# Filter matmuls behind the last scan: single PSUM banks, and products and projections in runs of fixed order

## Chip, cores and metric

One Trainium2 chip, one of its cores. The metric is the device time of the kernel in microseconds (us), from the first to the last instruction. Engines are named as in the profile: PE (TensorE), ACT (ScalarE), DVE (VectorE), POOL (GpSimd), SP (the queue that issues all the DMAs here).

## What is computed

Two layers on x of shape 4 x 64 x 64 x 128, all in float32. Layer 0: a state-space block that scans each image in four directions, then a mixture of experts. Layer 1: a mixing of rows and columns, then a spectral filter. Only the last is touched. Cut to what matters:

```python
Vf = jnp.fft.rfft(phi, n=8192, axis=0)                  # 16 filters
Uf_p = jnp.fft.rfft(u, n=8192, axis=1)
Uf_m = jnp.fft.rfft(u * sgn3, n=8192, axis=1)
U_plus  = jnp.fft.irfft(Vf[None,:,:,None] * Uf_p[:,:,None,:], ...)[:, :sl]
U_minus = ... * sgn
out = jnp.einsum('btkd,k,kde->bte', U_plus, s, Mpp)     # projection per filter
out = out + jnp.einsum('btkd,k,kde->bte', U_minus, s, Mpm)
```

So for each of 4 images u (4096 x 128), sixteen causal convolutions, each followed by a 128 x 128 projection, and the sum of all that.

## The kernel before

**Stages.** The four images go one after another through a scan (the loop from L1308 on), which keeps DVE and POOL busy. Beside each scan, pieces of other work are dealt out, 24 of the 64 filter groups among them. The rest is done behind the last scan, in the *tail* (L1412 to L1440).

**The filter.** Time is cut into blocks of 32, and a transform over blocks (`to_slots`) turns the convolution into small independent products in 64 frequency slots. `convolve` (L1053) works on a *group* of four slots of one image. For each group there are four *parts*: two halves `kq` of the 16 filters, times `e` = 0 and 1 (even and odd outputs). A part loads one *slab* of filter windows (four DMAs of 256 KB, L1075) and makes eight *products* (L1097): 64 rows of contraction, so that slot `q` = 0 uses rows 0 to 63 of the PE array and `q` = 1 rows 64 to 127; 512 columns, a full PSUM bank each. A bank pair is copied to SBUF (`y0` or `y1`) by `evict` (L232), in the tail by DVE and ACT in turn. After both `e` of a half, sixteen *projections* (L1116, 128 rows, 512 columns) add up in one bank `zq_ps`: eight read `y0` (weights `me`), eight read `y1` (`mo`). I call this unit (two parts: 16 products and 16 projections) a *half-group*. After two of them POOL adds, PE transposes four times (L1138, `zt_ps`), and the result goes to DRAM for `from_slots` (L1163), which transforms back and writes the output.

**The tail.** 40 groups are left, 80 half-groups. Stage 1 of the tail runs 24 of them beside `first_stages` (the last image's `after_scans`, `experts_and_sums`, `to_slots`); stage 2 runs the last image's 16 groups beside `from_slots` of two images; then `from_slots` of the last image alone. The loop at L1433 takes a piece of the stage, adds its weight times a ratio (3.2 or 18) to `due`, and takes filter pieces until their weights reach `due`. A filter piece is what lies between two `yield`s of `convolve`: two products and a copy (weight 4), or one projection (weight 2).

**Order and buffers.** [...]that order is made by a list scheduler at build time, from dependencies and its own estimates: it moves PE instructions of the filter and of the other stage past each other. PSUM has eight banks; in the tail `slots(4, 2)` makes four single banks (`bank`) and two pairs (`pair`); the products use the pairs, everything else the singles. Slabs have two buffers (`cp` has bufs=2); part i+1's slab is loaded during part i.

Of the kernel before, what the change touches and what calls it, by code (L numbers as in the profile page):

```python
# [10 lines left out]
F32 = mybir.dt.float32  # L11
# [6 lines left out]
P = 128  # L18
# [23 lines left out]
BS = 32  # L42
NB = HALF // BS
NQ = NB
KQ = 8
# [31 lines left out]
def kernel(  # L77
# [127 lines left out]
    side = {"tail": False}  # L205

    def slots(ones, twos):
        if "pool" in side:
            side["pool"].close()
        side["pool"] = ExitStack()  # L210
        for name, n in (("ones", ones), ("twos", twos)):
            side[name] = n and side["pool"].enter_context(
                tc.tile_pool(name=f"side_{name}", bufs=n, space=PSUM)
            )

    def bank(shape, name):

        if side["ones"]:
            return side["ones"].tile(shape, F32, name=name, tag="ps")
        n = int(np.prod(shape[1:]))  # L220
        ap = pair(name)[0 : shape[0], 0, 0:n]
        if len(shape) == 2:
            return ap
        sizes = {f"d{i}": d for i, d in enumerate(shape[1:])}
        names = " ".join(sizes)
        return ap.rearrange(f"p ({names}) -> p {names}", **sizes)

    def pair(name):

        return side["twos"].tile([P, 2, 512], F32, name=name, tag="ps2")  # L230

    def evict(dst, src):  # L232

        side["n"] = side.get("n", 0) + 1
        if side["tail"] and side["n"] % 2:
            nc.vector.tensor_copy(dst, src)  # L236
        else:
            nc.scalar.copy(dst, src)  # L238
# [7 lines left out]
    def later(pieces, work):  # L246
        put_off.append([pieces, work])

    def tick():
        for item in list(put_off):  # L250
            item[0] -= 1
            if item[0] <= 0:
                put_off.remove(item)
                item[1]()
# [798 lines left out]
    def convolve(groups, pool=None):  # L1053


        if not side["tail"]:
            slots(0, 1)
        with tc.tile_pool(name="cv", bufs=2) if pool is None else nullcontext(pool) as cp:
            parts = [(b, G, kq, e) for b, G in groups for kq in range(KF // KQ) for e in range(2)]
            us, slab = {}, {}  # L1060

            def load(i):
                b, G, kq, e = parts[i]
                if kq == 0 and e == 0:
                    us[b, G] = cp.tile([P, 2, 2, C], F32, name="us")
                    nc.sync.dma_start(
                        us[b, G],
                        ud[b][4 * G : 4 * G + 4].rearrange("(p q) r s a c -> (q r s) p a c", p=2),
                    )

                slab[i] = cp.tile([P, 2, 2, KQ, 2 * BS], F32, name="slab")
                half = KQ * 2 * BS * 2
                for qr in range(4):
                    off = (4 * G * 2 + qr) * (HDQ // 2) + (kq * 2 + e) * half
                    nc.sync.dma_start(  # L1075
                        slab[i][qr * BS : (qr + 1) * BS].rearrange("s p r k x -> s p (r k x)"),
                        bass.AP(
                            hd.tensor, hd.offset + off, [[1, BS], [2 * HDQ, 2], [1, half]]
                        ),
                    )  # L1080

            load(0)
            yield LAG
            zt, ys = {}, {}
            for i, (b, G, kq, e) in enumerate(parts):
                if i + 1 < len(parts) and e == 0:
                    load(i + 1)
                y = cp.tile([P, 2, 4, 2, KQ, BS], F32, name=f"y{e}", bufs=1)
                ys[e] = y
                for a in range(2):  # L1090

                    off = 1 - a if e == 1 else 0
                    for p in range(2):
                        ps = pair("cv_ps").rearrange("p q (r k t) -> p q r k t", r=2, t=BS)
                        for q in range(2):
                            rows = slice(q * 2 * BS, (q + 1) * 2 * BS)
                            nc.tensor.matmul(  # L1097
                                ps[:, q],
                                us[b, G][rows, p, a if e == 0 else 1 - a, :],
                                slab[i][rows, p, :, :, off : off + BS],  # L1100
                                start=True,
                                stop=True,
                            )
                        evict(
                            y[:, a, 2 * p : 2 * p + 2].rearrange("p q r k t -> p q (r k t)"),
                            ps.rearrange("p q r k t -> p q (r k t)"),
                        )
                        yield 4.0
                if e == 0:
                    continue  # L1110
                z = bank([P, 2 * 4 * 2, BS], "zq_ps")
                for e in range(2):
                    if i + 1 < len(parts) and e == 1:
                        load(i + 1)
                    for k in range(KQ):
                        nc.tensor.matmul(  # L1116
                            z,
                            (me, mo)[e][:, KQ * kq + k, :],
                            ys[e][:, :, :, :, k, :].rearrange("p a q r t -> p (a q r) t"),
                            start=(e == 0 and k == 0),  # L1120
                            stop=(e == 1 and k == KQ - 1),
                        )
                        if not (e == 1 and k == KQ - 1):
                            yield 2.0
                zt[kq] = cp.tile([P, 2, 4, 2 * BS], F32, name=f"zt{kq}", bufs=1)
                evict(zt[kq].rearrange("p a q n -> p (a q n)"), z.rearrange("p n t -> p (n t)"))
                yield 2.0
                if kq == 0:
                    continue

                def gather(b=b, G=G, z0=zt[0], z1=zt[1]):
                    nc.gpsimd.tensor_add(z0, z0, z1)  # L1132

                    def turn():
                        ps = bank([P, 2, 2, C], "zt_ps")
                        for p in range(2):
                            for a in range(2):
                                nc.tensor.transpose(  # L1138
                                    ps[:, p, a, :],
                                    z0[:, a, 2 * p : 2 * p + 2, :].rearrange("e q n -> e (q n)"),  # L1140
                                    ident,
                                )
                        zo = cp.tile([P, 2, 2, C], F32, name="zo", bufs=1)
                        evict(zo, ps)
                        later(
                            4,
                            lambda: nc.sync.dma_start(
                                zd[b][4 * G : 4 * G + 4].rearrange(
                                    "(p q) r t a c -> (q r t) p a c", p=2
                                ),  # L1150
                                zo,
                            ),
                        )

                    later(3, turn)

                later(2, gather)
            yield LAG
            flush()
        if not side["tail"]:  # L1160
            slots(2, 0)
# [42 lines left out]
    def run(pieces):  # L1204
        for _ in pieces:
            tick()
        flush()
# [21 lines left out]
    with ExitStack() as c0:  # L1229
# [51 lines left out]
        traced = nc.cur_bb.bb.instructions  # L1281
        order = mybir.DependencyInfo(mybir.DependencyClass.NoSync, mybir.DependencyReason.DATA)
# [25 lines left out]
        for s in range(-5, total + 2):  # L1308
            i = max(s, 0) // N

            t = s + 5
# [8 lines left out]
            t = s + 3  # L1320
# [11 lines left out]
            if 0 <= s < total:  # L1332
                b, k, step, _ = chunks[i]
# [76 lines left out]


    side["tail"] = True  # L1412
    slots(4, 2)

    def first_stages():
        yield from after_scans(B - 1)
# [8 lines left out]
    with tc.tile_pool(name="cv_tail", bufs=2) as cp:  # L1425

        for stages, groups, ratio in (
            (first_stages(), all_groups[BESIDE * (B - 1) : last], 3.2),
            (back(), all_groups[last:], 18.0),
        ):  # L1430
            filtered = convolve(groups, cp)
            due = made = 0.0
            for weight in stages:  # L1433
                tick()
                due += weight * ratio
                while made < due:
                    made += next(filtered, 1e9)
                    tick()
            run(filtered)
    run(from_slots(B - 1))  # L1440
    side["pool"].close()

# [73 lines left out]
```

## Time and profile before

The time is 11827.28 us, median of 3 runs (11826.74 to 11830.04).

| | us |
|---|---|
| span of the profiled run | 11825.1 |
| last scan instruction group ends, tail begins | 9376 |
| tail stage 1 (first stages beside filters) | 9376 to 10858 |
| tail stage 2 (back transforms beside filters) | 10858 to 11780 |
| last back transform alone | 11780 to 11825 |
| PE matmul records in the whole span | 34144 |

A float32 matmul leaves two records (passes) on PE, so the 80 half-groups of the tail show 2560 records at L1097 and 2560 at L1116. "Busy" in the group view is the union of the records' durations; their ends are modelled and reach into the next record, so I also use the distance from a record's start to the next record's start on PE, which adds up to the span.

### The profile page before, as it was taken

To read this page: it belongs to the slowest core of one execution; us is meant where nothing else is said; L and a number is where in the kernel's file an instruction comes from. 1 tells how busy PE (TensorE), PEld (TensorE's weight loads), DVE (VectorE), ACT (ScalarE), POOL (GpSimd) and SP (SyncE) were. 2 spreads that over 40 slices of the span, in tenths; PEclk is the share of its full clock that TensorE was granted. 3 is DMA by queue.
4 is the path that set the end of the run, shared out by engine and by line. 5 is a ranking of instruction groups with operands and counts; after the bars stand their busy time and mean duration, and the time that the engine had idled before them with its cause. 6 is when DMAs were issued, how large, how long until landed. Compare 5 with 4: busy or idle time off the path is not lost. (4 is left out here: it accounts for less than half of the span.)

```text
span 11825.1 us, 115511 instructions
## 1 busy us (share of the span) xinstructions
PE 8573.0 (72%) x34144; PEld 4828.5 (41%) x34144; DVE 8088.6 (68%) x6718; ACT 6138.8 (52%) x11666; POOL 7497.5 (63%) x6710
## 2 busy tenths in 40 slices
PE   6676675545766777557677775676677799999998
PEld 2444343333443334434544334454343333444333
DVE  0898888976976889868879897797798612122221
ACT  4656666656465555564655555646556433133111
POOL 1787788988776777877867779777677630011001
PEclk9787787656876888668778785786888799999999
DMA  2464556565645566647456556474665654534444
GB/s 100 159 206 163 195 170 212 192 189 156 237 155 171 175 188 181 192 141 245 158 177 185 173 176 195 167 241 140 191 190 174 179 134 127 131 99 115 109 106 107
DMA packets 901449, 1980.03 MB, mean 167 GB/s; under 512 B 101562, under 2 KB 415578, under 8 KB 899290
## 3 DMA queue, kind: packets, MB, share of 16 engines
q1 hardware_dynamic: 900826, 1972.65, 55.0%
q8 instruction: 278, 4.55, 0.2%
q14 instruction: 345, 2.83, 0.1%
HBM read 1766.77 MB, written 205.52 MB: 167 GB/s over the span
## 5 line engine op out<-in xcount | busy, mean ns | idle before, releaser
L1364 POOL TENSOR_TENSOR hh<-hh,bc 128x1024 f32<-128x1024 f32 x2048 | 4827.7, 2358 | 478.0 <-DVE hh L1356 186.9
L1356 DVE TENSOR_TENSOR_SCAN hh<-da,hst,db 128x512 f32<-128x512 f32 x3584 | 4393.1, 1267 | 768.0 <-PE y L1390 362.2
L1390 PE MATMUL y<-ident,hh 128*128 128x128 f32 x16384 | 2862.3, 325 | 1502.4 <-POOL hh L1364 1365.3
L1325 ACT ACTIVATE da<-dl,aneg 128x512 f32<-128x512 f32 x4096 | 2768.5, 717 | 2148.5 <-DVE hh L1356 2120.3
L1390 PEld LDWEIGHTS y<-ident,hh 128*128 128x128 f32 x16384 | 2315.9, 168 | 2944.8 <-POOL hh L1364 1750.2
L1350 DVE TENSOR_TENSOR db<-du,bc 128x1024 f32<-128x1024 f32 x2048 | 2523.4, 1232 | 832.7 <-ACT du L1344 718.5
L1097 PE MATMUL cv_ps<-slab,us 64*128 64x512 f32 x4096 | 1397.7, 707 | 590.2 <-ACT y L238 218.9
L238 ACT COPY y<-cv_ps 128x1024 f32<-128x1024 f32 x700 | 704.3, 1007 | 1152.7 <-PE cv_ps L1097 1100.6
L236 DVE COPY y<-cv_ps 128x1024 f32<-128x1024 f32 x324 | 396.0, 1224 | 1252.7 <-PE cv_ps L1097 1218.5
L1116 PE MATMUL zq_ps<-y,me 128*128 128x512 f32 x2048 | 1021.5, 616 | 70.4 <-ACT y L238 59.9
L1363 POOL COPY hst<-hh 128x2 f32<-128x2 f32 x1792 | 338.6, 189 | 1103.8 <-DVE hh L1356 1009.4
L1116 PE MATMUL zq_ps<-y,mo 128*128 128x512 f32 x2048 | 976.0, 601 | 6.1 <-DVE y L236 4.8
L1097 PEld LDWEIGHTS cv_ps<-slab,us 64*128 64x128 f32 x4096 | 421.6, 206 | 1213.4 <-ACT y L238 370.4
L1132 POOL TENSOR_TENSOR zt<-zt,zt 128x512 f32<-128x512 f32 x64 | 81.0, 1266 | 955.8 <-ACT zt L238 528.6
L1356 DVE TENSOR_TENSOR_SCAN hh<-da,db 128x512 f32<-128x512 f32 x512 | 597.1, 1208 | 129.1 <-PE y L1390 57.0
L1255 PE MATMUL dt_ps<-dts,dtw 8*128 8x512 f32 x512 | 409.5, 901 | 276.0 <-ACT dl L1258 128.1
L385 PE MATMUL cv_ps<-xh,diag 128*128 128x512 f32 x1152 | 541.1, 613 | 1.4 <-ACT xh L378 1.4
L1116 PEld LDWEIGHTS zq_ps<-y,me 128*128 128x128 f32 x2048 | 349.4, 194 | 429.4 <-issue 342.7
L1116 PEld LDWEIGHTS zq_ps<-y,mo 128*128 128x128 f32 x2048 | 359.1, 192 | 313.4 <-issue 298.5
L1264 POOL TENSOR_TENSOR ex<-ex,dx 128x1024 f32<-128x1024 f32 x128 | 302.6, 2364 | 162.1 <-ACT dx L1263 162.1
L1194 POOL TENSOR_TENSOR xr<-xr,iv 64x256 f32<-64x256 f32 x128 | 88.6, 719 | 412.0 <-ACT iv L1189 318.8
L385 PEld LDWEIGHTS cv_ps<-xh,diag 128*128 128x128 f32 x1152 | 215.5, 198 | 223.0 <-issue 220.8
(217 smaller groups left out, 8720.1 us busy)
## 6 DMA issues: line engine op xcount, KB each, us to landing
bc<-bc_d SPq DMA_DIRECT2D x2048, 512.0 KB
slab<-hd SPq DMA_DIRECT2D x1024, 256.0 KB
xc<-xc_d SPq DMA_DIRECT2D x128, 512.0 KB
y_d<-ys SPq DMA_DIRECT2D x128, 512.0 KB
w1t<-in_w_dram SPq DMA_DIRECT2D x128, 512.0 KB
w2t<-in_w_dram SPq DMA_DIRECT2D x256, 256.0 KB
xc_x<-xc_d SPq DMA_DIRECT2D x64, 512.0 KB
yk<-y_d SPq DMA_DIRECT2D x128, 256.0 KB
```

The lines of the kernel that those rows point to most:

```text
L236: nc.vector.tensor_copy(dst, src)
L238: nc.scalar.copy(dst, src)
L385: nc.tensor.matmul(ps, diag[:, h, t, :], xh[:, 8 * g + dy : 8 * g + dy + 8, dx : dx + W], start=(t == 0), stop=(t == 8),)
L1097: nc.tensor.matmul(ps[:, q], us[b, G][rows, p, a if e == 0 else 1 - a, :], slab[i][rows, p, :, :, off : off + BS], start=True, stop=True,)
L1116: nc.tensor.matmul(z, (me, mo)[e][:, KQ * kq + k, :], ys[e][:, :, :, :, k, :].rearrange("p a q r t -> p (a q r) t"), start=(e == 0 and k = ...
L1255: nc.tensor.matmul(ps, dtw[:, k, h * P : (h + 1) * P], dts, start=True, stop=True)
L1325: i_act = nc.scalar.activation(das[t][:, h, :], sizes[t // N][0][:, h, :], AF.Exp, scale=aneg[:, tk, h, t % N : t % N + 1],)
L1350: nc.vector.tensor_mul(db, dus[i], bcs[s][:, 0:1, :].to_broadcast([P, 2, SC]))
L1356: i_dve = nc.vector.tensor_tensor_scan(o, d0, d1, init, ALU.mult, ALU.add)
L1363: nc.gpsimd.tensor_copy(hsts[t // N][:, :, t % N], hhs[t][:, :, last])
L1364: i_pool = nc.gpsimd.tensor_mul(hhs[t], hhs[t], bcs.pop(t)[:, 1:2, :].to_broadcast([P, 2, SC]))
L1390: i_pe = nc.tensor.matmul(ys[c][:, q, h, :], hhs[t][:, h, q * P : (q + 1) * P], ident, is_transpose=True, start=(n == 0 and k > 0 and q % ...
```

## The change

In the tail only (`side["tail"]`), the changed kernel

- makes all eight PSUM banks single (`slots(8, 0)`): a product takes one bank, and each bank is copied by itself (512 columns in place of 1024), by DVE and ACT in turn;
- gives the products weight 0, so that all eight of a part are emitted without anything of the other stage between them, and each projection weight 4;
- adds ordering edges on PE (`behind`): each filter instruction stands behind the filter instruction before it, and other stages' PE instructions behind the last filter instruction emitted before them, so the scheduler no longer reorders the filters;
- loads slabs two parts ahead, into three buffers;
- puts the transposes of a finished group off by 12 pieces in place of 3.

```diff
-                slab[i] = cp.tile([P, 2, 2, KQ, 2 * BS], F32, name="slab")
+                slab[i] = cp.tile(
+                    [P, 2, 2, KQ, 2 * BS], F32, name="slab", bufs=3 if side["tail"] else 2
+                )
...
             load(0)
+            if side["tail"]:
+                load(1)
...
-                if i + 1 < len(parts) and e == 0:
+                if side["tail"]:
+                    if i + 2 < len(parts):
+                        load(i + 2)
+                elif i + 1 < len(parts) and e == 0:
                     load(i + 1)
...
-                        ps = pair("cv_ps").rearrange("p q (r k t) -> p q r k t", r=2, t=BS)
+                        ps = None if side["tail"] else pair("cv_ps")
+                        pq = [bank([P, 512], "cv_ps") if ps is None else ps[:, q] for q in range(2)]
+                        to = y[:, a, 2 * p : 2 * p + 2].rearrange("p q r k t -> p q (r k t)")
...
-                        yield 4.0
+                        if side["tail"]:
+                            for q in range(2):
+                                evict(to[:, q], pq[q])
+                            yield 0.0
+                        else:
+                            evict(to, ps)
+                            yield 4.0
...
-                    if i + 1 < len(parts) and e == 1:
+                    if i + 1 < len(parts) and e == 1 and not side["tail"]:
                         load(i + 1)
...
-                            yield 2.0
+                            yield 4.0 if side["tail"] else 2.0
...
-                    later(3, turn)
+                    later(12 if side["tail"] else 3, turn)
...
-    slots(4, 2)
+    slots(8, 0)
+    last_pe = []
+
+    def behind(start, filters):
+        for ins in traced[start:]:
+            if ins.engine == mybir.EngineType.PE:
+                if last_pe:
+                    tc.add_manual_dep(ins, last_pe[-1], order, reason="queued behind")
+                if filters:
+                    last_pe.append(ins.name)
...
+            start = len(traced)
             for weight in stages:
                 tick()
+                behind(start, False)
+                start = len(traced)
                 due += weight * ratio
                 while made < due:
                     made += next(filtered, 1e9)
                     tick()
+                behind(start, True)
+                start = len(traced)
             run(filtered)
+            behind(start, True)
```

More of the change, by code (lines that the diff above doesn't have):

```diff
@@ L1097, in convolve @@
                             nc.tensor.matmul(
-                                ps[:, q],
+                                pq[q].rearrange("p (r k t) -> p r k t", r=2, t=BS),
                                 us[b, G][rows, p, a if e == 0 else 1 - a, :],
@@ L1103, in convolve @@
                             )
[L1104 to L1107, printed above, removed]
-                        yield 4.0
+                        if side["tail"]:
[5 more added lines that the diff above has]
+                            yield 4.0
                 if e == 0:
```

## The prediction

> **What bounds the kernel now.** I read the page first. Its second part, the span in 40 slices, has two regimes:
>
> ```profile
> PE   6676675545766777557677775676677799999998
> DVE  0898888976976889868879897797798612122221
> ...
> PEclk9787787656876888668778785786888799999999
> ```
>
> Up to slice 31 DVE is the busy engine (the scans). In the last eight slices PE is full, DVE little used, and PE's clock is whole. The order of the two built programs is the same on every engine up to that tail, so only the tail from 9376 us on is at stake, 2449 us. The busy times by stretch cut it at its stages; after the stretch and its length come PE, weight load, DVE, ACT, POOL, then clock, DMA share and GB/s:
>
> ```profile
> 9376.00:10858.00 1482.00, 1373.72 (x4667) 599.44 (x4668) 306.74 (x293) 463.33 (x1087) 235.57 (x469) 0.97 0.49 123
> 10858.00:11780.00 922.00, 882.97 (x2298) 331.81 (x2296) 184.28 (x164) 171.76 (x196) 65.82 (x81) 0.99 0.44 107
> 11780.00:11825.00 45.00, 21.84 (x32) 5.06 (x32) 0.00 (x0) 10.94 (x16) 22.05 (x32) 0.73 0.74 185
> ```
>
> PE is busy 93 to 96% in both stages, so only cheaper PE time can help. The groups of the tail say where it goes (busy, mean ns of one, idle before and its releasers):
>
> ```profile
> L1097 PE MATMUL cv_ps<-slab,us 64*128 64x512 f32 x2560 | 821.2, 643 | 100.8 <-ACT y L238 47.3 <-DVE y L236 34.1 <-DMA slab<-hd 17.9
> L1116 PE MATMUL zq_ps<-y,me 128*128 128x512 f32 x1280 | 606.8, 610 | 16.8 <-DVE y L236 10.1 <-ACT y L238 6.7
> L1116 PE MATMUL zq_ps<-y,mo 128*128 128x512 f32 x1280 | 573.3, 596 | 6.1 <-DVE y L236 4.8 <-ACT y L238 1.1
> ```
>
> From start to start, the products take 897 us, the projections 1164, all else 380: 2441. A projection record takes 0.43 us (16 of them from 11174.04 to 11181.00), and 2560 x 0.43 = 1101, so projections are near their floor. For the products I went to the timeline of PE (start, length, instructions, records):
>
> ```profile
> 9878.62 1.99 PE L1097 MATMUL cv_ps<-slab,us 64*128 64x512 f32 x8
> 9881.10 1.99 PE L1097 MATMUL cv_ps<-slab,us 64*128 64x512 f32 x8 [0.49 <-DVE y L236]
> 9883.56 2.10 PE L1097 MATMUL cv_ps<-slab,us 64*128 64x512 f32 x8 [0.47 <-DVE y L236]
> 9886.15 1.99 PE L1097 MATMUL cv_ps<-slab,us 64*128 64x512 f32 x8 [0.49 <-DVE y L236]
> ...
> 11191.63 2.02 PE L1097 MATMUL cv_ps<-slab,us 64*128 64x512 f32 x4
> 11193.58 1.12 PE L1116 MATMUL zq_ps<-y,me 128*128 128x512 f32 x2
> 11194.64 1.99 PE L1097 MATMUL cv_ps<-slab,us 64*128 64x512 f32 x8
> 11196.56 2.84 PE L1116 MATMUL zq_ps<-y,me 128*128 128x512 f32 x6
> ```
>
> Eight records (four products) take 1.92 us to the next start, and four records (two products) 1.95. In the eight, records start two at a time, 7 ns apart, then 0.53 and 0.43 us on: both row halves of the array work at once. In the four they start one after the other. The built order explains it: there the scheduler put two products of the same half together, then others, then two of the other half; 83 of the 312 product runs of the tail are such "aa" or "bb". And a long run stalls 0.5 us after every four products, with two bank pairs to write.
>
> **What the skill says.** "TensorEngine Tiling (Array Packing)", section Key Properties: tiles work independently, and changing the tiling mode drains the engine. The trace agrees with both: 7 ns between halves, and the start after a change between L1097 and L1116 comes after 0.52 us in place of 0.43, so 0.09 each. The same page, PSUM Bottleneck: a faster tiled PE can leave the copies as the bound, and ScalarE and VectorE should share them. "TensorE: Matmul & The Clock Gate", The cost: per-tile semaphore tail: each product that counts up a semaphore costs about 26 ns at the end of a set. The change doubles these counts; no run here shows that price, and at 1280 products it is at most 17 us for the 640 added.
>
> **The change, part by part.**
>
> *Products in runs of 16.* In the changed built order 79 of 80 half-groups have one run of 16, halves strictly alternating (one is cut into 2, 1 and 13). Eight pairs of two passes: 0.53 + 14 x 0.43 + 0.53 = 7.08 us; x 80 = 566. Removed: 897 - 566 = **331 us**.
>
> *Can the copies follow?* Copies of one bank are in the trace: `zt` 586 ns on ACT, 692 on DVE. Per pair of products (0.86 us) each of the two makes one, so 0.69 fits, with little to spare. Depth: a first product ends 1.12 us after the run starts (0.53 + 0.59), a copy follows some 0.1 later and is done by 1.95; the bank is wanted by the fifth pair at 3.5. The slack is 1.5 us. Copies of 512 cost more per column (two on ACT 1.17 against 1.01), but lie under 13.8 us of projections, in which no copy is due. In stage 2 I therefore book no wait. `y0` and `y1` have one buffer each: their last readers are the projections ahead of the run, done on PE before it, so no wait.
>
> *Projections.* 80 x 32 x 0.43 = 1101. They are now broken by stage instructions in some 270 places and by products in 80, x 0.09 = 32: 1133. Removed: 1164 - 1133 = **31 us**.
>
> *All else* stays in number: 380.
>
> *Slabs two ahead.* 2 MB per half-group in about 21 us is 100 GB/s, and 25 to 60 for the rest; the page shows up to 245 GB/s in a slice. A slab is asked for once the part before last is done, some 20 us ahead of use. SP stands behind the store of `zo` at times, which comes five projections into the next half-group; a slab's four issues take 1.7 us and it lands some 5 later (the chain has 5 to 7 us at `slab<-hd`), before the need. The 17.9 us of slab waits are mostly the first load (14.7 us at 9399), which stays. Booked at nothing, but not safe.
>
> *The added order.* A stage's PE instruction now stands at a fixed place among the projections; if its input is late, all filters behind it wait, and with them the copies and the next slabs. Before, the stage instructions of stage 1 waited for next to nothing (idle 0.0 at most of their lines). I book: 12 us where `to_slots` of the last image now stands alone between the stages (its 16 matmuls and the DMA round trip have no filter beside them in the built order; before, they were mixed); 9 us where DVE's `top` and `rest` (4.4 us each) stand between copies of one run; 25 us for about eight runs in which the norm sums of ACT (0.3 to 0.5 us each, a dozen or more) stand between the copies and use up the 1.5 us slack, 3 us each; 13 for slabs and semaphores. Together **59 us**.
>
> Sum: 11827 - 331 - 31 + 59 = 11524; I say **11525 us**, and 11465 if the 59 vanish.
>
> **Rivals.**
>
> *The copies or the order bind in stage 1.* For it: ACT is busy there 463 of 1482 us, in order, waiting on POOL for each norm, and filters now cannot be moved around a late input. Against: eight banks in place of two pairs, and nearly no stage waits before. If every one of the 48 half-groups of stage 1 loses 3 us more: 11525 + 144 = about 11670.
>
> *The DMA takes over.* For it: a slab now has 21 us in place of 26, experts' weights come in stage 1 beside it. Against: DMA share 0.44 to 0.49. At 26 us per half-group in stage 2 nothing of its 170 us (half of the gain) is left: about 11695.
>
> *The halves do not overlap* (slower). Each product now waits for its own bank; if the second half always started after the first had ended, 16 products would take 16 x 0.86 = 13.8 us, x 80 = 1101, 204 more than now: 11827 + 204 - 31 + 59 = about 12060. Against: pairs with waits on different semaphores for each product (both satisfied) already start 7 ns apart.
>
> *It comes out better than the sum*: stage waits of before (some 40 us in the 380) shrink too: about 11440.
>
> **Chances.** Forecast 0.74; stage 1 binds 0.13; DMA 0.05; halves apart 0.03; better 0.05. The range reaches from 11455 (the 59 gone, a little of the waits too) to 11640 (most of stage 1's rival). Faster 0.96, same 0.01, slower 0.03.
>
> **What would show it.** Right: L1097 with 2560 records at some 570 to 600 us from start to start, runs of 32 records in 7.1 us; a half-group of stage 2 in 21 to 22 us in place of 27; copies at 0.59 and 0.69; PE still above 93% in stage 2. Wrong: PE idle before L1097 for y copies of over 60 us (rival one), for slabs over 30 (two), records of L1097 0.43 apart singly (three). A PE clock below 0.95 in the tail would also break it.

## The result and the profile after

The changed kernel takes 11536.91 us (median of 4 runs, 11531.63 to 11545.08); the kernel before, on the same chip, 11828.66 us (11826.74 to 11833.45). The ratio is 0.9753, with a 95% interval of 0.9736 to 0.9770. Predicted were 11525 us (11455 to 11640). The page's slices after, the same three rows as before:

```profile
PE   6676676545666677646767776566767779999998
DVE  0898888886886889967878889688789962222222
...
PEclk9687787656777888767778887677788889999999
```

The picture is that of before, with the full-PE regime one slice shorter. Busy time by stretch (stretch, length, then PE, weight load, DVE, ACT, POOL, clock, DMA share, GB/s), cut where the first filter of stage 2 starts and at the last back transform:

```profile
9376.00:10761.00 1385.00, 1321.84 (x4800) 617.68 (x4800) 355.75 (x503) 492.58 (x1291) 242.05 (x473) 0.97 0.55 139
10761.00:11484.00 723.00, 715.89 (x2176) 302.57 (x2176) 193.45 (x280) 185.69 (x312) 64.40 (x80) 0.99 0.52 122
11484.00:11529.00 45.00, 22.27 (x32) 5.25 (x32) 0.00 (x0) 10.91 (x16) 22.04 (x32) 0.73 0.75 186
```

PE is now busy 95% of stage 1 and 99% of stage 2 (93 and 96% before), and the DMA share rose by the shorter time only (0.49 to 0.55, 0.44 to 0.52; over both stages the rates and times give the same bytes). Stage 2 is shorter by more than the rate says, because of where it is cut: in the changed kernel stage 1's half-groups are all done there, while before, 16 products and 32 projections of stage 1 and 21 of the 32 passes of `fu_ps` still lay behind the cut at 10858. The groups of the tail (busy, mean ns, idle before and its releasers):

```profile
L1127 PE MATMUL zq_ps<-y,me 128*128 128x512 f32 x1280 | 598.9, 605 | 2.5 <-DVE y L236 2.5
L1106 PE MATMUL cv_ps<-slab,us 64*128 64x512 f32 x2560 | 595.0, 607 | 40.7 <-ACT no_sq L277 14.3 <-DMA us<-ud 10.7 <-ACT zt L238 8.1
L1127 PE MATMUL zq_ps<-y,mo 128*128 128x512 f32 x1280 | 584.3, 598 | 0.2 <-ACT y L238 0.2
```

The 81 us of waits for `y` copies ahead of the products are gone from this list. What is left of the idle time ahead of the products is the tail's first product (14.3), the first after `to_slots` (10.7), and 15.7 us elsewhere. The timeline of PE in stage 2 shows what the products have become (start, length, records):

```profile
10988.28 7.18 PE L1106 MATMUL cv_ps<-slab,us 64*128 64x512 f32 x32
10995.39 5.42 PE L1127 MATMUL zq_ps<-y,me 128*128 128x512 f32 x12
11000.65 0.60 PE L1149 MATMUL zt_ps<-ident,zt 128*128 128x128 f32 x4
11001.08 1.88 PE L1127 MATMUL zq_ps<-y,me 128*128 128x512 f32 x4
11002.80 7.03 PE L1127 MATMUL zq_ps<-y,mo 128*128 128x512 f32 x16
11009.76 7.18 PE L1106 MATMUL cv_ps<-slab,us 64*128 64x512 f32 x32
...
11032.86 7.18 PE L1106 MATMUL cv_ps<-slab,us 64*128 64x512 f32 x32
```

Sixteen products, 32 records, then the next start 7.11 us on (10988.28 to 10995.39); a half-group takes 21.5 us (10988.28 to 11009.76, with the transposes of `zt_ps` in it) or 23.1 (to 11032.86, with `gi_ps` of `from_slots`), in place of about 27.

Added up over the tail from one record's start on PE to the next record's start:

| us | before | after | measured | predicted |
|---|---|---|---|---|
| products | 897.4 | 607.5 | -290 | -331, and +47 of added waits |
| projections | 1163.6 | 1143.7 | -20 | -31 |
| `fu_ps` (`to_slots`, the junction of the stages) | 9.8 | 36.3 | +27 | +12 |
| all other | 347.0 | 326.0 | -21 | 0 |
| sum | 2417.8 | 2113.5 | -304 | -303 |

The sum came out within 2 us, partly by luck: three of its terms were off and cancelled. One thing that the prediction had at nothing is spread over these rows: the trace shows stretches of the tail in which PE's granted clock is 0.50 in place of 1.00 and a pass takes 0.86 us in place of 0.43. They add up to 135 us before and 110 after, and half of PE's busy time in them, an estimate of what they cost, is 42.5 us before and 30.8 after; in the products alone 28.6 and 10.4. By that estimate some 12 of the 304 us come from the clock, in one profiled run each; what moves the clock is not shown here.

The span has another source of scatter: the last scan ends on PE at 9384.5 us before and 9393.4 after, and between 9381.5 and 9400.8 over all the kernels below, though nothing up to there was edited. From that point to the end the tail takes 2440.6 us before and 2135.9 after. I give this *tail* beside each time from here on; it comes from one profiled run each, while the times have intervals.

### The profile page after: what moved, and what is told of

It is laid out like the page before. It is cut to its first block, busy times and chain, and to the rows that moved or that the text cites. A ratio compares the mean times of both kernels' runs of the same rounds, so it can differ in the third digit from the quotient of the medians.

```text
span 11529.3 us, 116175 instructions
## 1 busy us (share of the span) xinstructions
PE 8359.0 (73%) x34144; PEld 4814.5 (42%) x34144; DVE 8136.4 (71%) x7038; ACT 6172.0 (54%) x11986; POOL 7488.7 (65%) x6710
## 5 line engine op out<-in xcount | busy, mean ns | idle before, releaser
L1106 PE MATMUL cv_ps<-slab,us 64*128 64x512 f32 x4096 | 1172.2, 684 | 542.0 <-ACT zt L238 196.1
L238 ACT COPY y<-cv_ps 128x512 f32<-128x512 f32 (+1 forms) x1024 | 755.4, 741 | 643.2 <-PE cv_ps L1106 614.2
L236 DVE COPY y<-cv_ps 128x512 f32<-128x512 f32 x640 | 441.8, 691 | 633.1 <-PE cv_ps L1106 599.0
L236 DVE COPY zt<-zq_ps 128x512 f32<-128x512 f32 x37 | 25.6, 691 | 493.4 <-PE zq_ps L1127 487.7
```

Source lines behind the costliest of these rows:

```text
L1106: nc.tensor.matmul(pq[q].rearrange("p (r k t) -> p r k t", r=2, t=BS), us[b, G][rows, p, a if e == 0 else 1 - a, :], slab[i][rows, p, :, : ...
```

## Experiments

The theory: the gain comes from PE's own time, because runs of 16 products with strictly alternating halves and a bank each keep both row halves of the array full, and the copies can just follow. Rivals for the cause: the banks alone do it, whatever the order; the fixed order alone does it; the slabs loaded earlier do it; the copies are in fact the limit. None of the kernels leaves out any of the work. Their numbers, with ratio and 95% interval against the kernel before on the same chip; "products" and `fu_ps` are start to start over the tail:

| kernel | time, us | ratio | tail | products | `fu_ps` |
|---|---|---|---|---|---|
| changed | 11536.9 | 0.9753 (0.9736 to 0.9770) | 2135.9 | 607.5 | 36.3 |
| e1_order_alone | 11737.7 | 0.9926 (0.9911 to 0.9940) | 2348.4 | 816.0 | 35.4 |
| e2_banks_alone | 11550.8 | 0.9768 (0.9752 to 0.9784) | 2159.0 | 659.8 | 10.9 |
| e3_slab_one_ahead | 11549.1 | 0.9765 (0.9750 to 0.9779) | 2161.9 | 623.0 | 35.9 |
| e4_turn_after_3 | 11545.8 | 0.9759 (0.9744 to 0.9773) | 2154.8 | 617.6 | 36.8 |
| e5_halves_apart | 11676.8 | 0.9874 (0.9854 to 0.9893) | 2287.3 | 766.1 | 35.6 |
| e6_copies_on_dve | 11521.8 | 0.9742 (0.9728 to 0.9757) | 2132.4 | 604.1 | 35.9 |
| e7_ratio_3 | 11511.3 | 0.9729 (0.9713 to 0.9746) | 2118.6 | 608.2 | 18.4 |
| e8_ratio_prime | 11498.2 | 0.9724 (0.9709 to 0.9738) | 2112.2 | 608.4 | 15.1 |
| e9_prime_dve | 11494.1 | 0.9716 (0.9702 to 0.9731) | 2104.3 | 604.3 | 15.1 |
| e10_banks_slabs | 11518.5 | 0.9737 (0.9720 to 0.9753) | 2127.9 | 629.3 | 10.8 |
| e11_prime_dve_free | 11520.7 | 0.9741 (0.9725 to 0.9757) | 2128.6 | 630.9 | 14.4 |

### The order alone

Against the kernel before: the pairs stay (`slots(4, 2)`, one copy of 1024 columns), slabs one ahead, transposes after 3 pieces; added are only the weights and the edges.

```diff
-                        yield 4.0
+                        yield 0.0
-                                yield 2.0
+                                yield 4.0 if side["tail"] else 2.0
+    def behind(start, filters):   # as in the change, called in the loop of the tail
```

> The changed kernel with the copies in bank pairs again (four singles, two pairs), slabs one part ahead and the transposes put off by 3: of the change only the fixed order and the weights are left. My theory (bank depth and adjacent halves both needed): a product run stalls some 0.5 us before every second pair, as the run at 9878 us did (9.45 us for 16 products), so 80 x (9.45 - 7.11) = 187 us over the changed kernel's 11537: about 11725. Rival 'the fixed order carries the gain': at most 11570. Rival 'the banks carry it all': about 11820.

Measured: 11737.7 us, tail 92 us shorter than before. The halves now alternate in every run (a run is a row of products with no other PE work between), but the two pairs hold the products up; its products:

```profile
L1101 PE MATMUL cv_ps<-slab,us 64*128 64x512 f32 x2560 | 696.4, 646 | 153.3 <-DVE y L236 66.4 <-ACT y L238 58.9 <-DMA slab<-hd 15.7
```

125 us of waits for copies (81 before). A run of 16 takes 9.50 us in place of 7.11; 42 half-groups have one, the other 38 have their run cut by transposes. So the long runs without the banks bring less than a third of the tail's gain.

### The banks alone

```diff
-    slots(4, 2)
+    slots(8, 0)
-                        ps = pair("cv_ps")...; evict(<both>, ps)
+                        pq = [bank([P, 512], "cv_ps") for q in range(2)]
+                        for q in range(2): evict(to[:, q], pq[q])
```

Old weights, no edges, slabs one ahead, transposes after 3 pieces.

> Eight single banks and copies of one bank only; weights, slabs, put-off and the scheduler's freedom as before. Its built order has 199 product runs in the tail, all of them strictly alternating between the halves, none of the 83 same-half runs of the kernel before. My theory (what counts is that both halves work at once, and that a run finds free banks): counted by slots of 0.86 us and 0.2 per run the products take 594 us against 568, so about 11537 + 26 + 0 to 20 = 11565 to 11585. Rival 'the fixed order carries the gain': 11750 or more.

Measured: 11550.8 us, better than expected; the tail is 281.6 us shorter than before, so the banks, with copies bank by bank, bring 92% of the 304.7 without the order. The order is not needed to keep the halves alternating: with single banks the scheduler left 199 product runs in the tail, of 1 to 16 products, and in each the halves alternate; all the "aa" and "bb" runs are gone, as the expectation had read from the built order. Why the scheduler makes them with pairs and not with single banks stays open. So does what it is about the banks that helps with the waits for copies: the products can now take any of eight banks in place of two pairs, and each bank comes free by itself; no run separates the two. Both edits, the banks and the order, remove the "aa" and "bb" runs, so their gains (92 and 282) don't add up.

### One slab ahead, and the transposes after 3 pieces

```diff
-                    ... name="slab", bufs=3 if side["tail"] else 2   # and load(i + 2)
+                    ... name="slab", bufs=2                          # and load(i + 1), as before
```

> The changed kernel with slabs in two buffers and loaded one part ahead, as before. My theory (a slab is asked for some 14 us before its use even so, and lands in about 5 to 7): within 15 us of 11537. Rival 'the two-ahead load is needed': product runs wait for slab DMA by 1 us or more each, 11620 or more.

```diff
-                    later(12 if side["tail"] else 3, turn)
+                    later(3, turn)
```

> The changed kernel with a group's four transposes put off by 3 pieces, not 12. In the built order they now stand inside a product run (after 6 of 16 products) in some 38 of 40 groups. My theory: each costs a break (0.2 us) and a wait for POOL's addition (1.3 us behind the copy of the last projections, about 2.5 us after the run starts, while six products take 2.7): 38 x 0.3 to 1 us, 11545 to 11575. Rival 'no effect': 11537 within 5.

Measured: 11549.1 and 11545.8 us; the first within the 15 us of its expectation, the second at the low end, and neither separated from the changed kernel by its interval alone. In the tails, +26 and +19 us. Of e3's, +15.5 lie in the products and +9 in the projections, a spread of small waits; the wait for slabs itself is small, and 14.8 us of it stand ahead of the tail's first product:

```profile
L1101 PE MATMUL cv_ps<-slab,us 64*128 64x512 f32 x2560 | 595.9, 607 | 51.8 <-DMA slab<-hd 18.6 <-ACT y L238 16.0 <-issue 10.3
```

18.6 us of slab waits, about what the kernel before had (17.9). So the loads are worth some tens of microseconds at most.

### Is it the overlap of the halves?

The same work on the same banks, but each part makes its four products of one half and then four of the other, and the copies follow in that order.

```diff
+                    for q in range(2):
+                        for a in range(2):
+                            for p in range(2): nc.tensor.matmul(banks[4 * q + 2 * a + p] ...)
```

> The changed kernel, but each part emits its four products of rows 0-63 first and its four of rows 64-127 then (aaaabbbb in place of abababab). Same records, same number of copies, same run length. My theory: equal halves in a row go one after the other, and only a change of half overlaps: a run takes about 11.2 us in place of 7.1, 80 x 4.1 = 328: about 11865, slower than before. Rival 'run length and banks, not the alternation': 11540 to 11560.

Measured: 11676.8 us. Less overlap costs half of the gain (151 of the 305 us of tail are lost, with banks and order kept), so the overlap counts. But a run takes 9.19 us, not the expected 11.2: my model of the overlap was too strict. The records of the first products of one such run, from the trace (start us, duration ns):

```
11011.410 693   11011.943 589      first product
11012.372 589   11012.802 589      second
11013.231 589   11013.660 589      third
11013.237 693   11013.770 589      a product of the other half, begun 6 ns after the third
11014.089 589   11014.518 589      fourth, begun 0.85 us after that
```

In the queue the first product of the other half stands behind all four. It starts while the fourth is still waiting for its half: read so, because the "aa" and "bb" runs of the kernel before start pass by pass, 0.43 to 0.55 us apart. The copies support the reading, since they follow the order of the queue: the one of that product, whose passes end by 11014.36, starts only at 11015.19, just after the one of the fourth (11015.14), whose passes end at 11015.11. So the start passes the fourth product, and the report that it is done does not. All 79 long runs show both. So only the first two products of a run and the last two are alone: 1.82 us, six overlapping pairs in 5.57, 1.80, together the 9.19. The Trainium skill, "TensorE: Matmul & The Clock Gate", Part 3 (The mechanism), has matmuls start strictly in program order; these starts don't agree with that, and the measurement decides. Its "TensorEngine Tiling (Array Packing)", Key Properties (tiles work independently) agrees: 6 ns between two halves again.

### Are the copies near their limit?

```diff
-                            for q in range(2):
-                                evict(to[:, q], pq[q])
+                            for q in range(2):
+                                nc.vector.tensor_copy(to[:, q], pq[q])
```

> The changed kernel with all product copies on DVE (16 per run at 0.69 to 0.75 us in place of 8 on each engine). My theory (eight banks absorb half a run, the projections give the copies 13.9 us): the last product waits for the eighth copy, so a run takes some 8.2 us in place of 7.1: +88 us, less up to 40 us, since copies no longer stand behind ACT's norm sums: 11585 to 11625. Rival 'the copies' rate sets the pace': a run takes 16 x 0.75 = 12 us, +390: about 11930.

Measured: 11521.8 us, a miss: all copies on one engine, and the kernel is no slower. A run in stage 2, first PE, then DVE (start, length, instructions):

```profile
11020.65 7.21 PE L1106 MATMUL cv_ps<-slab,us 64*128 64x512 f32 x32
...
11021.81 9.66 DVE L1115 COPY y<-cv_ps 128x512 f32<-128x512 f32 x16 [0.29 <-PE cv_ps L1106]
```

Sixteen copies in 9.66 us, started every 0.598 us (11022.418, 11023.015, 11023.613 and so on), though each is recorded as 0.68 to 0.69 us long. I had taken 0.75 us for one, from pairs of copies that carried a wait in between. With 0.598 the eighth copy is done about 1.16 + 8 x 0.6 = 6 us after the run's start; eight banks let PE go on, and its run takes 7.144 us in place of 7.11. The rest of the copies lie under the projections. The skill's advice in "TensorEngine Tiling (Array Packing)", PSUM Bottleneck, to share the copies between ScalarE and VectorE, is not needed here: one engine nearly suffices, and ACT's norm sums can no longer hold product copies up.

### The junction of the stages

In the changed kernel `to_slots` of the last image stands between the two stages with no filter beside it. PE in that place:

```profile
10712.39 7.03 PE L1127 MATMUL zq_ps<-y,mo 128*128 128x512 f32 x16
10719.35 5.41 PE L1042 MATMUL fu_ps<-ub,fu_t 64*128 64x512 f32 x12
10724.70 0.66 PE L1149 MATMUL zt_ps<-ident,zt 128*128 128x128 f32 x4
10730.59 13.99 PE L1042 MATMUL fu_ps<-ub,fu_t 64*128 64x512 f32 x16 [5.23 <-DMA ub<-u_d]
10747.06 3.75 PE L1042 MATMUL fu_ps<-ub,fu_t 64*128 64x512 f32 x4 [2.49 <-DMA ub<-u_d]
10761.49 9.45 PE L1106 MATMUL cv_ps<-slab,us 64*128 64x512 f32 x32 [10.68 <-DMA us<-ud]
```

42 us pass from 10719 to 10761; 32 records of `fu_ps` would need 32 x 0.43 = 14. It is not the waits alone. Two windows of 5 us (stretch, length, then PE, weight load, DVE, ACT, POOL, clock, DMA share, GB/s):

```profile
10719.00:10724.00 5.00, 5.00 (x12) 2.16 (x12) 2.07 (x3) 1.23 (x3) 1.26 (x1) 1.00 0.51 116
10730.00:10735.00 5.00, 4.41 (x6) 1.78 (x7) 0.69 (x1) 0.58 (x1) 0.00 (x0) 0.50 0.53 150
```

The granted clock is 0.50 from 10728.5 to 10766.0, and 20 of the 32 passes start 0.86 us apart: 20 x 0.43 = 8.6 us more. Two kernels mend this junction: one takes a smaller ratio in stage 1, so that three half-groups are left over and stand among the pieces of `to_slots`; the other also asks for each stage's first two slabs ahead of the stage's own loads, and so starts the filters a little sooner.

```diff
-            (first_stages(), all_groups[BESIDE * (B - 1) : last], 3.2),
+            (first_stages(), all_groups[BESIDE * (B - 1) : last], 3.0),
```

> The changed kernel with the first ratio at 3.0 in place of 3.2, so that three half-groups of filters are left when the last image's to_slots begins. In the changed kernel's trace PE spends 42 us between 10719 and 10761 on 14 us of to_slots matmuls and transposes. My theory (that gap is a chain of DMA round trips that filters can lie beside): -25 to -30 us, about 11510. Rival 'stage 1 is bound by the first stages' own chain': the same wait appears elsewhere, 11535.

```diff
-            due = made = 0.0
-            start = len(traced)
+            start = len(traced)
+            due = made = next(filtered)
+            behind(start, True)
+            start = len(traced)
```

> As the ratio of 3.0, and the first slabs of each filter stage are asked for ahead of the stage's own first loads. My theory: the first product waits some 14 us behind the last scan for a slab whose request stands behind six y loads on the DMA queue (3.9 us of issue): 4 us less, about 11506. Rival 'the first slab waits for buffers of the scan': as without it.

Measured: 11511.3 and 11498.2 us, tails 17 and 24 us below that of the changed kernel. At the junction of e7:

```profile
10665.47 2.84 PE L1127 MATMUL zq_ps<-y,me 128*128 128x512 f32 x6
10668.24 1.98 PE L1042 MATMUL fu_ps<-ub,fu_t 64*128 64x512 f32 x4
10670.15 4.56 PE L1127 MATMUL zq_ps<-y,me 128*128 128x512 f32 x10
```

`fu_ps` now stands between projections and takes 18.4 us in all (36.3); the stretch at a clock of 0.50 lasts 10.2 us here and 6.8 in e8, in place of 37.5. In e8 the tail's first product comes 9.6 us after the last scan, in place of 14.3.

### What the fixed order is worth

The change without weights and edges: single banks, slabs two ahead, transposes after 12 pieces.

```diff
-                            yield 0.0
+                            yield 4.0
-                                yield 4.0 if side["tail"] else 2.0
+                                yield 2.0
-        for ins in traced[start:]:
+        for ins in []:
```

> The change without its fixed order and its new weights: eight single banks, slabs two parts ahead, turns of 12, stage and filter instructions mixed by the scheduler (177 product runs in the built order instead of 79, halves still alternating in each). If the banks and the slabs carry the gain, the tail lies between the banks alone (2159 us) and the changed kernel (2136 us), less the 15 to 26 us that the slabs cost when one part ahead: about 2137 to 2145 us, time 11530 to 11545. If the fixed order is needed to keep the long runs full, the tail stays at 2155 us or above and the time at 11550 or above. If the fixed order costs more than it brings (the junction of 36 us at fu_ps against 11 with the scheduler), the tail falls below 2130 us and the time below 11525.

Measured: 11518.5 us, tail 2127.9: the third branch. Without its order the change is as fast or faster; the tail by 8 us, while the intervals of the two ratios overlap.

```profile
L1106 PE MATMUL cv_ps<-slab,us 64*128 64x512 f32 x2560 | 625.1, 610 | 25.3 <-DMA slab<-hd 17.1 <-ACT y L238 5.6 <-DVE y L236 1.2
```

More busy, less idle: 177 runs in place of 82, and each run costs 7.11 - 16 x 0.43 = 0.23 us beyond its passes, at its two ends, where the shape changes (a run of two products in this kernel 0.20). 95 x 0.23 = 22, and the products are 629.3 - 607.5 = 22 us longer. Against that, the projections are 8 us shorter, and `fu_ps` 25.5. The scheduler had mixed the junction by itself.

The best parts together: e8 with all product copies on DVE; and then the same with the order taken away again.

```diff
-                                evict(to[:, q], pq[q])
+                                nc.vector.tensor_copy(to[:, q], pq[q])
```

> Three half-groups left for the hand-over, first slabs asked for ahead of the last stages' loads, and all product copies on DVE. If the wins are independent, the time is that of the version with the first two (11498) less what the DVE copies brought alone (15): about 11483, tail 2105 to 2110 us. If the DVE copies only took back stalls that also vanish otherwise, it stays at 11495 to 11505.

```diff
-                            yield 0.0
+                            yield 4.0
-                                yield 4.0 if side["tail"] else 2.0
+                                yield 2.0
-        for ins in traced[start:]:
+        for ins in []:
```

> The kernel of e9_prime_dve (11494 us, tail 2104) with the fixed order and the new weights taken away, as in e10_banks_slabs. From the changed kernel against e10, the order brings 22 us in products and costs 8 in projections and 26 at the junction; in e9 the junction already has other work (15 us from start to start at fu_ps in place of 36), so there the order costs only some 4 there. If these terms carry over, the order is worth about 10 us here: tail 2112 to 2118 us, time 11500 to 11508. If the scheduler's mix is as good in every case (the order is worth nothing with single banks), the time stays at 11488 to 11497. If it is better by as much as in e10, below 11485.

Measured: e9 11494.1 us, tail 2104.3, the fastest of all; its interval (0.9702 to 0.9731) lies below that of the changed kernel. The tail (2105 to 2110 expected of independent gains) is just below that range, the time between the two theories. e11 takes 11520.7 us, more than its expectation: the order is worth 24 us of tail there, not some 10. The products are 26.6 us longer without it (22 expected) and the projections 10.8 shorter, but the junction gives nothing back (14.4 against 15.1), and all other work takes 8 us more. Part of the 24 us is the granted clock: half of PE's busy time at 0.50 is 25.0 us in e11 and 15.8 in e9, by the estimate used above; the rest of the 8 us has no one cause that was found. Priming, ratio and DVE copies without the order bring nothing (2128.6 against 2127.9). So the order pays once its junction is mended (some 24 us of tail in one profiled run each, about 9 of them clock), and not as the change has it.

## Why the prediction was right

- **Products in runs of 16** (566 us at 7.08 each). Right: 79 runs of 32 records, median 7.11 us. The sum is 79 x 7.11 = 562, 8 for the half-group that is cut up, and 37.5 us of excess in twelve runs: 607.5. Booked for such waits were 9 + 25 + 13 = 47. The semaphore counts did not double: in the trace before, 755 of the tail's 1280 products already counted up, now all do. They cost at most the 0.03 us that 7.11 is above 7.08, 2.4 us in 80 runs; the prediction's estimate was up to 17.
- **Where the excess lies.** As booked, in stage 1 (eleven runs) and in the first run after the junction, mostly behind ACT's norms. Not booked was the clock: by the estimate above some 10 of the 37.5 us are passes at 0.50, among them 3 of the 4.5 us of the first of the twelve runs and the 2.3 us of the last. ACT beside one run, from its timeline:

```profile
9488.43 0.20 ACT L285 ACTIVATE no_r<-no_r 128x2 f32<-128x2 f32 x1
9490.11 0.60 ACT L302 ACTIVATE yk<-yk,no_m,no_r 128x256 f32<-128x256 f32 x1 [1.48 <-POOL no_m L297]
9490.62 0.56 ACT L238 COPY zt<-zq_ps 128x512 f32<-128x512 f32 x1
...
9491.58 1.54 ACT L238 COPY y<-cv_ps 128x512 f32<-128x512 f32 x3
```

  ACT waits 1.48 us for POOL, and the copies of `zt` and `y` stand behind it; PE's eighth product of that run starts at 9491.23, after 5.28 us of idling. One run of 15.9 us comes out of this, some 2.5 us of it by the clock, which is 0.50 from 9489.4 to 9496.2.
- **The copies can follow.** Right, and by more than the step said: 0.598 us per copy when they stand close, not 0.69, and one engine does nearly all that two do. The booked slack was not what made it safe.
- **Projections** (1133). 1143.7, a term too small. From the distances of starts: 2560 x 0.429 = 1098, 21 us more at the ends of 302 rows of projections (waits included; there were to be 350 ends), 21 at their first records (189 of them take 0.1 more) and 3 elsewhere. The step charged each break once, at its end; it should have charged the beginning too, while the end costs nothing ahead of a 128 x 128 transpose (0.429) and 0.09 ahead of products and others of another shape (0.522). Of the 20 us by which the row fell, ten are two waits of 5 us ahead of `zt_ps` that are gone: these sums charge a wait to the record in front of it.
- **The junction** (+12). Too small: +26.5. Before, the passes of `fu_ps` lay beside products of the other rows (9.8 us for 32 passes that take 13.8 one by one). Now they stand alone (+4), 20 of them run at the clock of 0.50 (+8.6), and PE waits 2.5 us for `ub` and 10.7 for `us` (+13.2). A first wait of 5.2 us for `ub` falls in the row of all other, behind `zt_ps`. e7 and e8 show it by removing it.
- **All else** (0). -21: above all `zt_ps` (-9) and `yt_ps` (-3.5). Before, products stood behind 32 groups of transposes and waited there, 6.7 us in all, which the sums charge to `zt_ps`; now projections stand there. This is the rival "better than the sum", in part; it paid for the junction and the projections.
- **Slabs** booked at nothing: no new wait, as said. Loading one ahead costs 26 us of tail in the new kernel.
- **The rest of the 12 us.** The tail was predicted at -303 and came at -304.7. Median time less the tail of the profiled run is 9386 to 9393 us in the kernel before and the eleven experiments, and 9401 in the changed kernel, whose profiled run (11531.6) is itself 5.3 us below its median. So the missing 12 us lie mostly outside the tail, in the scatter of a part that the change leaves alone; why it scatters is open.
- **The cause.** The prediction was right that full row halves and copies that keep up make the products cheap (e1, e5, e6). It took the alternation from the changed built order, together with runs of 16, and did not ask which of the two edits makes it; the sum did not depend on that. e2 shows that single banks give it without the order, and e10 that the order as built nets about nothing.

## What to carry to other kernels

When products of a half array run one by one, first look for what keeps the second half from starting: here one bank per product, copied by itself, was worth 282 of 305 us, and a written order only some 25, and that only once the hand-over between the stages was filled with other work. A fixed order shows its price at the seams: look at the timeline where one stage ends and the next begins, and at the granted clock there. Read a copy engine's rate from the distance of starts in a row that is full, not from the length of single records.

## What was not expected of the hardware

- A product of the other row half starts together with the third of four products of one half, though the fourth stands ahead of it in the queue (6 ns apart; a run 9.19 us, not 11.2); its copy starts only after that of the fourth.
- Around the junction PE's granted clock is 0.50 for 37.5 us and passes start 0.86 us apart; with filters mixed in (e7 to e11) no such stretch there is longer than 10.2 us.
- DVE copies of 128x512 from PSUM start every 0.598 us in a row, while each one's record is 0.68 to 0.69 us long.
- The end of the last scan wanders from 9381.5 to 9400.8 us over kernels whose code up to there is unedited, more than several of the differences measured here.
